# Graph attention on one core: the order of lower and whole sums, steps and masks at the end of a head

## The chip, the cores and the metric

The kernel runs on 1 core of a Trainium2 chip. The metric is the time of one execution on the device, in microseconds (us); lower is better. Several runs of each kernel are made, and their median is given.

## The reference, cut to what matters

Two layers are computed on x (4096 x 256) with one adjacency matrix of 4096 x 4096. The first layer is one graph attention and 30 steps of a small feed-forward network; the second is two graph attentions and a mixture of experts. Each of the three attentions has 4 heads of 64 columns:

```python
h = jnp.einsum('nd,mdo->mno', x, W)
e = jax.nn.leaky_relu(f_src[:, :, None] + f_dst[:, None, :], LEAK)
e = jnp.where(adj[None, :, :] > 0, e, NEG_INF)
attn = jax.nn.softmax(e, axis=-1)
out = jax.nn.elu(jnp.einsum('mnk,mko->mno', attn, h))
```

The change touches only how the three attentions are ordered.

## The kernel before, in words

**The trick of the attention.** The exponential of a leaky ReLU of a sum of two terms is one of two products, by the sign of the sum. So a neighbour k contributes to a row n with one of two prepared vectors, and which one is a comparison of 0 and 1. The kernel needs no exponential of a 4096 x 4096 matrix: it needs masks of 0 and 1 and matmuls of those masks with the prepared vectors (`vals`, 65 columns in two precision parts, an upper and a lower, for each of the two branches: 260 columns).

**Tiles and loops.** The 4096 rows are cut into chunks: of 4, 7, 7, 7 and 7 tiles of 128 rows in the first attention, and of 8, 8, 8, 8 in the second and third. For each chunk and head there are 16 units (q), each with 2 tiles of 128 neighbours. The list `units` runs over chunks, heads and q. So the first attention has 20 heads (chunk times head), the others 16 each, 52 in all. For each unit:

- ScalarE makes two steps (L466, tile `st`): large where the sum is positive, 0 elsewhere.
- VectorE makes a first mask `m1` (L580) from the step and the adjacency mask, and in 10 of 16 units a second mask `m2` (L604) as the difference of the adjacency mask and `m1`. In the other 6 units (`turned`) the vectors are prepared so that no second mask is needed.
- TensorE multiplies the masks with `vals` (L546) and accumulates over the 16 units into two PSUM tiles, `acc0` (4 tiles of rows, or fewer in the first chunk) and `acc1` (the others).

At a head's end ScalarE takes the lower part out of each accumulator, scaled (`lo`, L474, the "lower sum"), and VectorE adds it to the upper part (`u`, L475, the "whole sum"). Only then can the next head accumulate into the same tile. Below, lo0 and W0 are the lower and the whole sum of `acc0`, lo1 and W1 those of `acc1`. Then `close` works the sums to the head's output, in six pieces spread over the units that follow (L483 to L498, L638 to L642). In the first attention, during all chunks but the last, GpSimd also issues loads of the adjacency matrix for the next chunk (L209), TensorE turns them (L219), VectorE compares them (L227, L229) and SP stores them.

**What sets the order.** The main loop over `at` is written out by hand for VectorE and ScalarE (`tc.manual_schedule`): these two engines run their instructions in the order of the code. TensorE's order is left to the scheduler, which follows the code closely. An iteration issues the steps of unit `at + LEAD` (LEAD is 2), the masks of unit `at`, and the products of unit `at - LAG` (LAG is 1 in the first attention, 2 in the others). The step tiles have 3 buffers in the first attention and 4 in the others, the `m1` tiles likewise, and each accumulator one. When `at - LAG` is the first unit of a head, the sums of the head before are issued in this iteration, by `take`, once for k = 0 and once for k = 1.

Of the kernel before, what the change touches and what calls it, by code (L numbers as in the profile page):

```python
# [11 lines left out]
F32 = mybir.dt.float32  # L12
BF16 = mybir.dt.bfloat16
F16 = mybir.dt.float16
I32 = mybir.dt.int32
AF = mybir.ActivationFunctionType
OP = mybir.AluOpType
# [4 lines left out]
P = 128  # L22
# [9 lines left out]
DV = D + 1  # L32
BIG = 2.0**60
SCALE = 2.0**-4
LOW = 2.0**11
# [9 lines left out]
def gnn_ffn_kernel(ctx: ExitStack, tc: tile.TileContext, a: dict, out: bass.AP):  # L45
    nc = tc.nc
# [41 lines left out]
    def rows_in():  # L88
        return stream.tile([P, G * C], F32, name="rows")
# [35 lines left out]
    def turned(q):  # L125
        return q % 3 == 0
# [45 lines left out]
    def attention(tag, src, norm, w, others, chunks, first, ends, following):  # L172
# [6 lines left out]
        CM = max(chunks)  # L179
        with ExitStack() as scope:  # L180
# [3 lines left out]
            f2b = lay.tile([P, NT, H], F32, name="f2b")  # L184
# [4 lines left out]
            end = None if first else scope.enter_context(tc.tile_pool(name=f"{tag}_end", bufs=1))  # L189
            masks, arow, f1b = {}, {}, {}  # L190
# [53 lines left out]
            with ExitStack() as ps:  # L244
                prep = ps.enter_context(tc.tile_pool(name=f"{tag}_prep", bufs=1))
                work = ps.enter_context(tc.tile_pool(name=f"{tag}_pw", bufs=2))
# [204 lines left out]
            if first:  # L451
                end = scope.enter_context(tc.tile_pool(name=f"{tag}_end", bufs=1))
                made = scope.enter_context(tc.tile_pool(name=f"{tag}_made", bufs=2))
            work = scope.enter_context(tc.tile_pool(name=f"{tag}_work", bufs=2))
# [3 lines left out]
            units = [(c, h, q) for c in range(len(chunks)) for h in range(H) for q in range(NJ)]  # L458
            steps, accs = {}, {}

            def step_of(c, h, q):

                w = chunks[c] * P
                st = steps[c, h, q] = work.tile([P, 2, CM * P], BF16, name="st", bufs=3 if first else 4)
                for s in range(2):
                    nc.scalar.activation(  # L466
                        st[:, s, :w], f1b[c, h][:, :w], AF.Relu, bias=f2b[:, 2 * q + s, h : h + 1], scale=BIG
                    )

            def take(u, i0, n, acc):  # L470

                both = acc[:, :n, : 4 * DV].rearrange("p i (b s c) -> p i b s c", b=2, s=2)
                lo = end.tile([P, 4, 2, DV], F32, name="lo", bufs=2)
                nc.scalar.activation(lo[:, :n], both[:, :, :, 1, :], AF.Copy, scale=1.0 / LOW)  # L474
                nc.vector.tensor_tensor(u[:, i0 : i0 + n], both[:, :, :, 0, :], lo[:, :n], OP.add)  # L475

            def close(c, h, u):

                nt, t0 = chunks[c], starts[c]
                begin, finish = ends  # L480
                more = begin(t0, nt, h, end)
                v = u[:, :, 0, :]
                nc.vector.tensor_tensor(  # L483
                    v[:, :nt], v[:, :nt], r[:, t0 : t0 + nt, h : h + 1].to_broadcast([P, nt, DV]), OP.mult
                )
                yield
                nc.vector.tensor_tensor(v[:, :nt], v[:, :nt], u[:, :nt, 1, :], OP.add)
                yield

                nc.vector.tensor_tensor(v[:, :nt], v[:, :nt], hs[:, :, h, :].to_broadcast([P, nt, DV]), OP.add)  # L490
                z = end.tile([P, CM, 1], F32, name="z", bufs=2)
                nc.vector.reciprocal(z[:, :nt], v[:, :nt, D : D + 1])
                yield
                o = v[:, :, :D]
                nc.vector.tensor_tensor(o[:, :nt], v[:, :nt, :D], z[:, :nt].to_broadcast([P, nt, D]), OP.mult)
                yield
                e = end.tile([P, CM, D], F32, name="e")
                nc.scalar.activation(e[:, :nt], o[:, :nt], AF.Exp)  # L498
                yield
                finish(t0, nt, h, o[:, :nt], e[:, :nt], more)  # L500
                yield
# [25 lines left out]
            LEAD, LAG = 2, 1 if first else 2  # L527
            pairs = {}
# [34 lines left out]
            closing, making = None, None  # L563
            with tc.manual_schedule(engines={mybir.EngineType.DVE, mybir.EngineType.Activation}):
                for at in range(LEAD):
                    step_of(*units[at])
                for at in range(len(units) + LAG):
                    if at < len(units):
                        c, h, q = units[at]
                        w = chunks[c] * P  # L570
                        if q == 0 and h == 0 and first and c + 1 < len(chunks):
                            making = make(c + 1)
                        if q == 4 and at + NJ < len(units):
                            load_f1(*units[at + NJ - 4][:2])
                        if at + LEAD < len(units):
                            step_of(*units[at + LEAD])
                        m = masks[c, q // 4][:, 2 * (q % 4) : 2 * (q % 4) + 2, :w]
                        st = steps.pop((c, h, q))
                        m1 = work.tile([P, 2, CM * P], BF16, name="m1", bufs=3 if first else 4)
                        nc.vector.tensor_tensor(  # L580
                            m1[:, :, :w], st[:, :, :w], m, OP.logical_and if turned(q) else OP.min
                        )
                        pairs[at] = [m, m1, None]
                    for k in range(2):
                        b = at - LAG
                        if b >= 0:
                            bc, bh, bq = units[b]
                            if bq == 0:
                                if b:
                                    pc, ph_ = units[b - 1][:2]  # L590
                                    if k == 0:
                                        u = end.tile([P, CM, 2, DV], F32, name="u")
                                    take(u, *accs[pc, ph_][k])
                                    if k == 1:
                                        closing = close(pc, ph_, u)
                                        accs.pop((pc, ph_))
                                space(bc, bh, k)
                            products(b, k)
                        if k == 0 and at < len(units) and not turned(q):
                            if first:  # L600
                                m2 = work.tile([P, 2, CM * P], BF16, name="m2")
                            else:
                                m2 = rows_in().bitcast(BF16).rearrange("p (s n) -> p s n", s=2)
                            nc.vector.tensor_tensor(m2[:, :, :w], m, m1[:, :, :w], OP.subtract)  # L604
                            pairs[at][2] = m2
                    if b >= 0:
                        pairs.pop(b)
                        if bh == H - 1 and bq % 4 == 3 and bc + 1 < len(chunks):
                            load_mask(bc + 1, bq // 4)
                        if bq in (1, 2, 3, 4, 6, 8) and closing is not None:  # L610
                            next(closing)
                    if making is not None:
                        next(making, None)
                    if at == len(units) - (8 if first else 4):
                        for g in range(3 if first else 2):
                            load_ahead(*following[:1], g, *following[1:])
            c, h, q = units[-1]
            u = end.tile([P, CM, 2, DV], F32, name="u")
            for k in range(2):
                take(u, *accs[c, h][k])  # L620
            for _ in close(c, h, u):
                pass

# [35 lines left out]
    with ExitStack() as scope:  # L659
        one = scope.enter_context(tc.tile_pool(name="f_one", bufs=1))  # L660
        wT = one.tile([P, KC, C], F32, name="wT")
        bias = one.tile([P, C], F32, name="bias")
        last = one.tile([P, C], F32, name="last")
        y = one.tile([P, NT, C], F32, name="y")
        work = scope.enter_context(tc.tile_pool(name="f_work", bufs=3))
# [61 lines left out]
        units = FFN_STEPS * NG  # L727
        for at in range(units + 4):
# [18 lines left out]
            if 0 <= at - 3 < units:  # L747
                u = at - 3
# [13 lines left out]
                end = u >= units - NG  # L762
# [30 lines left out]
    for i in range(2):  # L793
        at = 1 + i * KC * E
# [29 lines left out]
    with ExitStack() as scope:  # L824
# [5 lines left out]
        acc = one.tile([P, NT, C], F32, name="acc")  # L830
# [10 lines left out]
        with ExitStack() as rs:  # L841
            work = rs.enter_context(tc.tile_pool(name="r_work", bufs=2))
# [15 lines left out]
            for g in range(NG + 2):  # L858
# [12 lines left out]
                if 1 <= g <= NG:  # L871
                    u = g - 1
# [4 lines left out]
                    n = work.tile([P, G, C], F32, name="n")  # L877
# [8 lines left out]
                if 2 <= g:  # L886
                    u = g - 2
# [18 lines left out]
            def numbers(name, pattern, base, step, dtype=F32):  # L906
# [19 lines left out]
            before = rone.tile([P, P], F32, name="before")  # L926
            nc.gpsimd.memset(before, 1.0)
            nc.gpsimd.affine_select(
                before, before, pattern=[[1, P]], compare_op=OP.is_gt, fill=0.0, base=0, channel_multiplier=-1
# [66 lines left out]
            first = rone.tile([P, E], F32, name="first")  # L996
# [19 lines left out]
            lo = rone.tile([P, 2, NT], F16, name="lo")  # L1016
# [3 lines left out]
            for b in range(2 * NT // HB):  # L1020
                i, t0 = b // 2, b % 2 * HB
# [152 lines left out]
        for i in range(T + 1):  # L1174
# [9 lines left out]
            h = hT.pop(i, None)  # L1184
# [55 lines left out]
```

## Time and profile before

| | us |
|---|---|
| median of 3 runs | 3596.79 (3593.67 to 3600.78) |
| the profiled execution | 3587.08 |
| its span | 3585.3 |
| first attention, first lower sum to last | 151.8 to 833.9 |
| second attention, the same | 2050.3 to 2593.3 |
| third attention, the same | 2696.8 to 3244.5 |

The profile is of one execution, a little faster than the three runs. Its times of instructions are read from the start of the span. Engines are PE (TensorE), PEld (its weight loads), DVE (VectorE), ACT (ScalarE), POOL (GpSimd) and SP (SyncE). A group of instructions is named by its line, engine and operation, with output and inputs by the program's tile names; "idle before, releaser" is the time for which the engine had nothing to run in front of the instruction, and what ended it. The ends of matmuls are modelled, and neighbouring instructions on one engine overlap a little, so that starts are the safer numbers.

### The profile page before, as it was taken

What the parts mean: (1) busy time and instruction counts of PE and PEld (TensorE: products, weight loads), DVE (VectorE), ACT (ScalarE), POOL (GpSimd) and SP (SyncE); (2) the same over time, 40 slices, a digit from 0 to 9 for tenths busy, and PEclk for the clock granted to TensorE, in tenths of its full rate; (3) what the DMA queues carried; (4) which work ended last, traced back from release to release, by engine and by line L of the source; (5) the groups of instructions that cost most, each with busy time, mean ns of one, the idle gap of its engine ahead of it and who ended that gap; (6) DMA issues with size and microseconds to landing.
All of it is one profiled execution on the core that took longest, in us unless ns stands there. A gap on an engine that the chain in (4) does not pass through costs nothing. (4 is left out here: it accounts for less than half of the span.)

```text
span 3585.3 us, 80790 instructions
## 1 busy us (share of the span) xinstructions
PE 3265.5 (91%) x33523; PEld 2971.2 (83%) x33523; DVE 3013.9 (84%) x6039; ACT 2612.6 (73%) x2902; POOL 1101.1 (31%) x899
## 2 busy tenths in 40 slices
PE   6789999987999999999998899999979999996895
PEld 5688888886888888888887799999868999994784
DVE  6789999987877877877787799999989999997445
ACT  2688888896766666666663799999879999993221
POOL 3210010003877777777772000000000000001663
PEclk8899999998999999999999899999999999998897
DMA  6796877601000000000006021303130331404224
GB/s 136 138 230 118 204 171 152 191 22 54 7 1 1 1 1 1 1 1 1 1 1 213 19 73 68 116 25 116 56 123 26 121 117 37 131 20 165 82 94 183
DMA packets 280199, 288.46 MB, mean 80 GB/s; under 512 B 97149, under 2 KB 230426, under 8 KB 279834
## 3 DMA queue, kind: packets, MB, share of 16 engines
q1 hardware_dynamic: 198770, 224.18, 18.9%
q0 software_dynamic: 73920, 52.97, 9.6%
q10 hardware_dynamic: 7144, 6.16, 0.6%
q8 instruction: 264, 4.33, 0.5%
q14 instruction: 101, 0.83, 0.1%
HBM read 248.01 MB, written 68.81 MB: 88 GB/s over the span
## 5 line engine op out<-in xcount | busy, mean ns | idle before, releaser
L546 PE MATMUL acc<-vals,m 128*128 128x130 f16 (+1 forms) x19456 | 1723.4, 233 | 138.1 <-DVE u L475 81.8
L466 ACT ACTIVATE st<-f1b,f2b 128x1024 bf16<-128x1024 f32 (+2 forms) x1664 | 1658.5, 1072 | 146.1 <-DVE m L580 138.2
L546 PEld LDWEIGHTS <-m 128*128 128x128 bf16 x19456 | 1525.2, 98 | 232.2 <-issue 85.7
L580 DVE TENSOR_TENSOR m<-st,m 128x2048 bf16<-128x2048 bf16 (+2 forms) x832 | 929.3, 1134 | 16.3 <-ACT st L466 12.4
L754 PE MATMUL po<-wT,zT 128*128 128x256 f32 x3840 | 875.2, 381 | 12.7 <-ACT zT L780 12.3
L754 PEld LDWEIGHTS po<-wT,zT 128*128 128x128 f32 x3840 | 714.0, 191 | 103.9 <-ACT zT L780 14.8
L740 POOL TENSOR_TENSOR th<-th,y 128x1024 f32<-128x1024 f32 x240 | 567.9, 2367 | 194.1 <-ACT th L739 193.5
L546 PE MATMUL acc<-vals,rows 128*128 128x130 f16 x5120 | 611.1, 221 | 0.0
L106 POOL TENSOR_TENSOR ln_rstd<-ln_rstd,mhalf 128x4 f32<-128x4 f32 x272 | 282.5, 1040 | 896.4 <-DVE ln_rstd L105 685.8
L101 DVE BATCH_NORM_STATS2 ln_st<-z 128x6 f32<-128x256 f32 x960 | 337.7, 413 | 191.3 <-ACT z L745 191.3
L546 PEld LDWEIGHTS <-rows 128*128 128x128 bf16 x5120 | 490.8, 96 | 0.4
L780 ACT COPY zT<-tp 128x1024 f32<-128x1024 f32 x240 | 243.0, 1012 | 323.8 <-PE tp L114 323.8
L604 DVE TENSOR_TENSOR rows<-m,m 128x2048 bf16<-128x2048 bf16 x320 | 391.7, 1224 | 10.2
L764 DVE SCALAR_TENSOR_TENSOR y<-po,ln_rstd,bias 128x256 f32<-128x256 f32 x928 | 378.2, 468 | 4.9 <-PE po L754 4.9
L745 ACT ACTIVATE z<-th 128x1024 f32<-128x1024 f32 x240 | 254.3, 1060 | 18.1 <-POOL th L740 17.8
L114 PE MATMUL tp<-ident,z 128*128 128x128 f32 x1920 | 250.8, 274 | 9.0 <-ACT z L745 8.0
L114 PEld LDWEIGHTS tp<-ident,z 128*128 128x128 f32 x1920 | 225.6, 141 | 35.7 <-ACT z L745 10.7
L739 ACT ACTIVATE th<-y 128x1024 f32<-128x1024 f32 x240 | 251.1, 1047 | 4.7 <-DVE y L764 4.7
L209 POOL DMA_DIRECT2D rows<-in_adj_dram x80 | 72.9, 912 | 510.1 <-PE tp_m L219 499.8
L604 DVE TENSOR_TENSOR m<-m,m 128x1792 bf16<-128x1792 bf16 (+1 forms) x200 | 202.2, 1011 | 12.7
L449 POOL MEMSET hs<- 128x4 f32 x3 | 0.3, 101 | 617.6 <-DVE u L490 596.4
L307 PE MATMUL ph<-g_w,xT 128*128 128x264 f32 x384 | 117.5, 469 | 31.1 <-DVE v L377 27.9
(212 smaller groups left out, 2312.9 us busy)
## 6 DMA issues: line engine op xcount, KB each, us to landing
m<-edges SPq DMA_DIRECT2D x32, 2048.0 KB, 9.8
rows<-in_adj_dram POOLq DMA_DIRECT2D x64, 448.0 KB, 7.1
edges<-ms SPq DMA_DIRECT2D x64, 448.0 KB, 5.1
m<-edges SPq DMA_DIRECT2D x16, 1792.0 KB
f1b<-fd SPq DMA_DIRECT2D x32, 512.0 KB, 3.5
rows<-x1d SPq DMA_DIRECT2D x16, 512.0 KB, 6.8
y<-yd SPq DMA_DIRECT2D x16, 512.0 KB, 9.0
f1b<-fd SPq DMA_DIRECT2D x16, 448.0 KB, 3.7
```

The source lines that it names most:

```text
L101: nc.vector.bn_stats(st[:, r, :], src[:, r, :])
L106: nc.gpsimd.tensor_tensor(rstd, rstd, mhalf, OP.pow)
L114: nc.tensor.transpose(ps[:, k, r * P : (r + 1) * P], src[:, r, k * P : (k + 1) * P], ident)
L466: nc.scalar.activation(st[:, s, :w], f1b[c, h][:, :w], AF.Relu, bias=f2b[:, 2 * q + s, h : h + 1], scale=BIG)
L546: nc.tensor.matmul(acc[:, i, cols], lhs[:, s, rows], v[:, cols], start=(j == 0 and n_ == 0), stop=(j == NT - 1 and n_ == 1), skip_group_ch ...
L580: nc.vector.tensor_tensor(m1[:, :, :w], st[:, :, :w], m, OP.logical_and if turned(q) else OP.min)
L604: nc.vector.tensor_tensor(m2[:, :, :w], m, m1[:, :, :w], OP.subtract)
L739: nc.scalar.activation(th[at], y[:, g * G : (g + 1) * G, :], AF.Tanh, scale=0.01)
L740: nc.gpsimd.tensor_tensor(th[at], th[at], y[:, g * G : (g + 1) * G, :], OP.add)
L745: nc.scalar.activation(z, th.pop(at - 1), AF.Silu, scale=0.01)
L754: nc.tensor.matmul(po[:, r, :], src[:, k, r * P : (r + 1) * P], wT[:, k, :], start=(k == 0), stop=(k == KC - 1),)
L764: nc.vector.scalar_tensor_tensor(y[:, g * G + r, :], po[:, r, :], rstd[:, r : r + 1], last if end else bias, op0=OP.mult, op1=OP.add,)
```

## The change

`take` is split in two, `lower_sums` (ScalarE) and `whole_sums` (VectorE), and `step_of` issues one step at a time. In the iteration of a head's end the order becomes:

| engine | before | after |
|---|---|---|
| ScalarE | step, step, lo0, lo1 | lo0, step, lo1, step |
| VectorE, first attention | m1, W0, m2, W1 | m1, W0, W1, m2 |
| VectorE, second and third | m1, W0, m2, W1 | W0, m1, W1, m2 |

In all other iterations the order is as before. The products of both halves are now written behind all of these. In the second and third attention this leaves TensorE's order as it was; in the first, at a head's start, the scheduler no longer puts the first matmuls of the second unit in front of `acc1`'s matmuls of the first. The orders of SP and GpSimd are the same. The number of buffers, the tiles and the arithmetic are unchanged, and so is the end of each attention behind the loop.

```diff
+                    b = at - LAG
+                    bc, bh, bq = units[b] if b >= 0 else (0, 0, -1)
+                    before = units[b - 1][:2] if b > 0 and bq == 0 else None
...
-                        if at + LEAD < len(units):
-                            step_of(*units[at + LEAD])
+
+                    los = []
+                    for k in range(2):
+                        if before:
+                            los.append(lower_sums(*accs[before][k]))
+                        step_of(at + LEAD, k)
+
+                    if before and not first:
+                        whole_sums(u, los[0], *accs[before][0])
...
                         pairs[at] = [m, m1, None]
-                    for k in range(2):
-                        b = at - LAG
-                        if b >= 0:
-                            bc, bh, bq = units[b]
+                    if before:
+                        if first:
+                            whole_sums(u, los[0], *accs[before][0])
+                        whole_sums(u, los[1], *accs[before][1])
+                        accs.pop(before)
+                        closing = close(*before, u)
+                    if at < len(units) and not turned(q):
...
+                        nc.vector.tensor_tensor(m2[:, :, :w], m, m1[:, :, :w], OP.subtract)
+                        pairs[at][2] = m2
+
+                    if b >= 0:
+                        for k in range(2):
                             if bq == 0:
-                                if b:
-                                    pc, ph_ = units[b - 1][:2]
-                                    if k == 0:
-                                        u = end.tile([P, CM, 2, DV], F32, name="u")
-                                    take(u, *accs[pc, ph_][k])
-                                    if k == 1:
-                                        closing = close(pc, ph_, u)
-                                        accs.pop((pc, ph_))
                                 space(bc, bh, k)
                             products(b, k)
-                        if k == 0 and at < len(units) and not turned(q):
...
-                            nc.vector.tensor_tensor(m2[:, :, :w], m, m1[:, :, :w], OP.subtract)
-                            pairs[at][2] = m2
```

The two functions that `take` was split into:

```python
def lower_sums(i0, n, acc):
    lo = end.tile([P, 4, 2, DV], F32, name="lo", bufs=2)
    nc.scalar.activation(lo[:, :n], split(acc, n)[:, :, :, 1, :], AF.Copy, scale=1.0 / LOW)
    return lo

def whole_sums(u, lo, i0, n, acc):
    nc.vector.tensor_tensor(
        u[:, i0 : i0 + n], split(acc, n)[:, :, :, 0, :], lo[:, :n], OP.add
    )
```

More of the change, by code (lines that the diff above doesn't have):

```diff
@@ L459, in attention, with step_of, split @@
             steps, accs = {}, {}
-            def step_of(c, h, q):
+            def step_of(at, s):
+                if at >= len(units):
+                    return
+                c, h, q = units[at]
                 w = chunks[c] * P
[L464 to L472, printed above, removed]
-                lo = end.tile([P, 4, 2, DV], F32, name="lo", bufs=2)
-                nc.scalar.activation(lo[:, :n], both[:, :, :, 1, :], AF.Copy, scale=1.0 / LOW)
-                nc.vector.tensor_tensor(u[:, i0 : i0 + n], both[:, :, :, 0, :], lo[:, :n], OP.add)
+                if s == 0:
+                    steps[at] = work.tile([P, 2, CM * P], BF16, name="st", bufs=3 if first else 4)
+                nc.scalar.activation(
+                    steps[at][:, s, :w], f1b[c, h][:, :w], AF.Relu, bias=f2b[:, 2 * q + s, h : h + 1], scale=BIG
+                )
+            def split(acc, n):
+                return acc[:, :n, : 4 * DV].rearrange("p i (b s c) -> p i b s c", b=2, s=2)
+            def lower_sums(i0, n, acc):
+                lo = end.tile([P, 4, 2, DV], F32, name="lo", bufs=2)
+                nc.scalar.activation(lo[:, :n], split(acc, n)[:, :, :, 1, :], AF.Copy, scale=1.0 / LOW)
+                return lo
+            def whole_sums(u, lo, i0, n, acc):
+                nc.vector.tensor_tensor(
+                    u[:, i0 : i0 + n], split(acc, n)[:, :, :, 0, :], lo[:, :n], OP.add
+                )
             def close(c, h, u):
@@ L565, in attention @@
                 for at in range(LEAD):
-                    step_of(*units[at])
+                    for s in range(2):
+                        step_of(at, s)
                 for at in range(len(units) + LAG):
+                    b = at - LAG
+                    bc, bh, bq = units[b] if b >= 0 else (0, 0, -1)
+                    before = units[b - 1][:2] if b > 0 and bq == 0 else None
+                    if before:
+                        u = end.tile([P, CM, 2, DV], F32, name="u")
                     if at < len(units):
@@ L574, in attention @@
                             load_f1(*units[at + NJ - 4][:2])
-                        if at + LEAD < len(units):
-                            step_of(*units[at + LEAD])
+                    los = []
[5 more added lines that the diff above has]
+                        whole_sums(u, los[0], *accs[before][0])
+                    if at < len(units):
                         m = masks[c, q // 4][:, 2 * (q % 4) : 2 * (q % 4) + 2, :w]
-                        st = steps.pop((c, h, q))
+                        st = steps.pop(at)
                         m1 = work.tile([P, 2, CM * P], BF16, name="m1", bufs=3 if first else 4)
@@ L583, in attention @@
                         pairs[at] = [m, m1, None]
-                    for k in range(2):
-                        b = at - LAG
-                        if b >= 0:
-                            bc, bh, bq = units[b]
-                            if bq == 0:
-                                if b:
-                                    pc, ph_ = units[b - 1][:2]
-                                    if k == 0:
-                                        u = end.tile([P, CM, 2, DV], F32, name="u")
-                                    take(u, *accs[pc, ph_][k])
-                                    if k == 1:
-                                        closing = close(pc, ph_, u)
-                                        accs.pop((pc, ph_))
+                    if before:
+                        if first:
[4 more added lines that the diff above has]
+                    if at < len(units) and not turned(q):
+                        if first:
+                            m2 = work.tile([P, 2, CM * P], BF16, name="m2")
+                        else:
+                            m2 = rows_in().bitcast(BF16).rearrange("p (s n) -> p s n", s=2)
+                        nc.vector.tensor_tensor(m2[:, :, :w], m, m1[:, :, :w], OP.subtract)
+                        pairs[at][2] = m2
+                    if b >= 0:
+                        for k in range(2):
+                            if bq == 0:
                                 space(bc, bh, k)
                             products(b, k)
-                        if k == 0 and at < len(units) and not turned(q):
[L600 to L604, printed above, removed]
-                            pairs[at][2] = m2
-                    if b >= 0:
                         pairs.pop(b)
@@ L619, in attention @@
             for k in range(2):
-                take(u, *accs[c, h][k])
+                whole_sums(u, lower_sums(*accs[c, h][k]), *accs[c, h][k])
             for _ in close(c, h, u):
```

## The prediction

> **What bounds the kernel now.** I read the page first (which engines are busy), then the table of windows for one head in each attention, then the timeline of one head's end, engine by engine, and last VectorE's list of waits by stage.
>
> The page's first part shows three engines close together, so no single one can be named from it:
> ```profile
> PE 3265.5 (91%) x33523; PEld 2971.2 (83%) x33523; DVE 3013.9 (84%) x6039; ACT 2612.6 (73%) x2902; POOL 1101.1 (31%) x899
> ```
> The windows below run from one first lower sum of a head to the next: the first attention, the second, the third. Columns: window, length, then busy us of TensorE, weight loads, VectorE, ScalarE, GpSimd, then clock, DMA share, GB/s.
> ```profile
> 424.88:463.17 38.29, 34.71 (x504) 32.32 (x504) 35.77 (x43) 32.18 (x36) 3.72 (x4) 1.00 0.64 122
> 2232.02:2268.13 36.11, 34.81 (x514) 33.35 (x512) 35.27 (x36) 35.10 (x36) 0.00 (x0) 1.00 0.08 24
> 2880.84:2917.22 36.38, 34.79 (x512) 33.33 (x512) 35.53 (x36) 35.09 (x36) 0.00 (x0) 1.00 0.11 31
> ```
> The reader is to see that VectorE works most in all three (35.77 of 38.29, 35.27 of 36.11, 35.53 of 36.38), and that the second and third attention have under 1.4 us of slack per head on any engine. What a head can win is what VectorE idles. The timeline of a head's end in the second attention (start, length, what, and in brackets the idle time before it and its releaser; ScalarE, then VectorE, then TensorE):
> ```profile
> 2227.87 4.25 ACT L466 ACTIVATE st<-f1b,f2b 128x1024 bf16<-128x1024 f32 x4
> 2232.03 1.07 ACT L474 ACTIVATE lo<-acc 128x520 f32<-128x520 f32 x2
> ...
> 2230.95 1.22 DVE L580 TENSOR_TENSOR m<-st,m 128x2048 bf16<-128x2048 bf16 x1
> 2232.64 0.70 DVE L475 TENSOR_TENSOR u<-acc,lo 128x520 f32<-128x520 f32 x1 [0.47 <-ACT lo L474]
> 2233.26 1.22 DVE L604 TENSOR_TENSOR rows<-m,m 128x2048 bf16<-128x2048 bf16 x1
> 2234.39 0.69 DVE L475 TENSOR_TENSOR u<-acc,lo 128x520 f32<-128x520 f32 x1
> ...
> 2229.25 2.84 PE L546 MATMUL acc<-vals,m 128*128 128x260 f16 x32
> 2233.39 1.56 PE L546 MATMUL acc<-vals,m 128*128 128x260 f16 x17 [1.30 <-DVE u L475]
> ```
> TensorE's last unit of the head runs 2229.25 to 2232.09; its first half of 16 matmuls (for acc0) is done 1.42 earlier, at 2230.67. The lower sum lo0 starts only at 2232.03, since the four steps before it fill ScalarE. So VectorE waits 0.47 and TensorE 1.30. VectorE's waits in the three attentions, in order (total us, times, longest):
> ```profile
> DVE u L475 <- ACT lo L474: 40.5, 20, 3.0
> ```
> ```profile
> DVE u L475 <- ACT lo L474: 14.1, 17, 3.8
> ```
> ```profile
> DVE u L475 <- ACT lo L474: 13.2, 16, 3.5
> ```
> That is 67.8 us in all: about 1.9 per head in the first attention, 0.47 and 0.45 in the others, except 3.1 at the first head's end of the second and third (timeline at 2050.9 and 2697.4). The last wait of each attention lies in the drain, where nothing is left to run: 3.0, 3.8 and 3.5 of the sum, and not to be won.
>
> **What the Trainium skill says.** "Trainium Architecture — The Big Picture", section "Inside one NeuronCore": every engine has an instruction stream of its own and meets the others only at semaphores. So the place of an instruction in its queue decides; the trace agrees (lo0 ready at 2230.67, run at 2232.03). "ScalarE: Activation LUTs", section "What ACT_TABLE_LOAD costs": an ACTIVATE with a pointer bias takes 280 ns + 0.833 ns per element, two in a row overlap by 93 ns: 1133 ns for a step of 1024, 1.04 us from start to start. The trace's median step is 1133 ns, and four take 4.25. "Perfetto Trace Analysis", section "Matmuls": groups should rotate through PSUM banks so that emptying one overlaps the next group. "PSUM — Partial Sum Buffer", section "PSUM: the matmul accumulator": 8 banks of 2 KiB a partition. Here acc0 and acc1 (4+4 tiles of 512 fp32) are all 8, so the only overlap is acc1's matmuls while acc0 is emptied.
>
> **The change part by part.** Nothing is added or removed: each engine has as many instructions as before, and the queues of SP and GpSimd keep their order. In the second and third attention TensorE's order stays too; in the first, at a head's start, the next unit's first few matmuls move behind those of acc1. What moves is 104 lower sums, 104 whole sums, the steps beside them, and the second masks (L604).
>
> *Second attention, a usual head.* ScalarE: lo0 moves past two steps, lo1 past one. The step in front of them ends at 2229.95 (two starts of 1.04 before 2232.03), so lo0 waits for TensorE until 2230.7 and ends at 2231.3; a step to 2232.3; lo1 (acc1 was done at 2232.09) to 2232.8; the other step to 2233.8. VectorE: W0 now stands ahead of the mask; 2231.3 to 2232.0, mask, W1 to 2233.8, second mask to 2234.9. TensorE starts at 2232.1 instead of 2233.39, and acc1 is free when it gets there. Already this first time the next mask starts at 2234.85 instead of 2235.00. From then on TensorE's head begins 1.1 us earlier against VectorE's queue: from W0's start it needs 0.70 + 0.06 + 33.4 (34.81 less the last half, 1.42) + 0.06 + 0.58 (lo0) + 0.03 = 34.8 us round to the next W0, ScalarE 35.1, VectorE 36.11 - 0.47 = 35.64. So VectorE sets the head, its wait is gone, and a head costs 35.64: **0.47 less**. ScalarE's wait for TensorE (0.75 at first) is hidden in what it already waits for buffers of VectorE (timeline: 0.72 at 2244.21, 0.93 per head in all).
>
> *Its first head's end.* lo0 comes 2.08 us (two steps) earlier, W0 at 2048.8 instead of 2050.86. The head after took 37.3, with 1.1 us in which VectorE waited for a buffer of the late TensorE; it takes 35.64 now. By the second head's end 3.7 us are won. With 13 more heads at 0.47: 3.7 + 6.1 = **9.8 us**.
>
> *Third attention.* In the same way: W0 2.08 earlier, the next head 38.56 down to 36.38 - 0.45 = 35.93: 4.7, and 13 x 0.45 = 5.9: **10.6 us**.
>
> *First attention.* There W0 stays behind the mask, and both whole sums come ahead of the second mask. Head end at 463 (chunks of 7 tiles): the step in front of lo0 ends 461.4, TensorE's acc0 at 461.4 (462.4 less 12 matmuls of 0.089), the mask 461.92. lo0 to 462.0, W0 462.03 to 462.73, a step, lo1 463.0 to 463.5, W1 463.5 to 464.06, second mask to 465.1, copy of the turned mask, next mask 465.53 instead of 466.41. VectorE's wait of 1.86 becomes 0.1 before W0 and 0.87 more before W1: **0.87 won**. TensorE starts at 462.9 instead of 464.54, and its next unit needs the second mask at 465.4, which is there at 465.1. The last chunk, which turns no masks, gives 0.93 by the same steps (wait 2.51 to 0.8 + 0.75), the first chunk's heads 0.58 and, where the chunk ends, 0.85. Sum: 3 x 0.58 + 0.85 + 11 x 0.87 + 4 x 0.93 = **15.9 us**. The last sums of each attention, which keep their order, I count at nothing: they wait for TensorE's last matmuls (ScalarE idle 5.7 us in front of lo0 at 832.9).
>
> The wait added: W1 waits for lo1, which stands behind a step, and the second mask is queued behind it, with TensorE's next unit waiting for that. It is 0.3 us early in the reckoning. The wait of a step behind lo0 isn't in the trace of before; its price lies between 0 (it replaces a wait for buffers) and 0.75 us per head. I take 0, since ScalarE has 1.0 us spare per head. DMA is not cover for anything: the share is 0.08 to 0.11 in usual heads of the later attentions; in a chunk's last head of the first attention it is 0.97, so four such heads might win nothing (3.5 us).
>
> **Sum:** 15.9 + 9.8 + 10.6 = 36.3 us. The profiled execution took 3587.08 (span 3585.3) and would take 3550.8; it was 9.7 under the median of 3596.79, so the median goes to **3560.5**.
>
> **The rivals.** (a) Main case as reckoned, gain 25 to 47: 0.70. (b) All of VectorE's waits for lower sums vanish, those before W1 too: 40.5 - 3.0, 9.7 + 0.6 and 9.1 + 1.6 (the buffer waits after the first heads), some 57 us, 3540. For it: TensorE would start 1.6 earlier per head. Against: lo1 stands behind a step of 0.94 in all of the first attention. 0.08. (c) Only the first attention wins, because in the others W0 ahead of the mask waits for TensorE as long as it did for ScalarE: 3596.8 - 15.9 = 3581. For it: 0.36 us of wait remains in the first reckoned head. Against: the loop over TensorE is 0.8 short of VectorE's. 0.10. (d) The wait is only handed on, from VectorE's sum to ScalarE's steps, and the head stays as long: no change, 3597. Over 1.0 us of spare time per head speaks against it. 0.05. (e) Slower, by one mechanism: lo0 blocks ScalarE until TensorE's acc0 is done, and the steps are queued behind it. ScalarE's head is 35.10 plus the stall; it decides from a stall of 1.01 us (second attention) or 1.29 (third), and outweighs the first attention's 15.9 from 1.7. With TensorE half a unit later (1.42) the stall is 2.14, a head 37.24, and 15 x 1.13 + 15 x 0.86 = 30 us are lost against 15.9 won: 3611. Against: TensorE is released earlier, not later. 0.07.
>
> **How the numbers follow.** About 0.2%, 7 us, is what a measurement of this kernel can tell from no change. (a), (b), (c) are faster: 0.88; (d) 0.05; (e) 0.07. The range 3538 to 3584 holds (a) and (b), (c), and some us of drift of the median (its runs span 7 us); it leaves out (d), (e) and some of the thinner gains.
>
> **What would show it.** Right: the wait of W0 near nothing in the later attentions, heads of 35.6 and 35.9 us there and some 37.4 in the first, TensorE's gap before a head under 1 us, ScalarE's lower sums with short waits for TensorE. Wrong: ScalarE busy 35.1 with waits over 1 us at lo0 and masks waiting for steps (e), or VectorE waiting 0.4 us and more before W0 in each later head (c), or TensorE waiting for the second mask after a head's start in the first attention.

## The result, and the profile after

The changed kernel took 3559.89 us (median of 4 runs, 3558.91 to 3561.31) against 3598.78 for the kernel before: a ratio of 0.9891, 95% interval 0.9873 to 0.9909. Measured again later, both kernels side by side, it was 3549.86 against 3583.46, a ratio of 0.9907 (0.9890 to 0.9924). About 1% is won, 34 to 39 us; 36.3 were predicted.

The page of the profile after, first part (busy us and share of the span, 3557.2 us):
```profile
PE 3272.9 (92%) x33523; PEld 2963.8 (83%) x33523; DVE 3010.9 (85%) x6039; ACT 2613.4 (73%) x2902; POOL 1101.7 (31%) x899
```
The work is the same, and the shares rose only because the span is shorter. The table of windows of the profile after, one head from lower sum to lower sum, in the first, second and third attention (window, length, busy us of PE, PEld, DVE, ACT, POOL, then clock, DMA share, GB/s):
```profile
414.94:452.34 37.40, 34.91 (x507) 32.27 (x506) 35.87 (x44) 32.28 (x35) 3.72 (x4) 1.00 0.64 125
2208.16:2243.71 35.55, 34.96 (x515) 33.34 (x514) 35.17 (x36) 35.10 (x35) 0.00 (x0) 1.00 0.09 24
2846.84:2882.65 35.81, 34.96 (x515) 33.32 (x514) 35.44 (x36) 35.10 (x35) 0.00 (x0) 1.00 0.11 31
```
A head fell from 38.29 to 37.40, from 36.11 to 35.55, from 36.38 to 35.81; VectorE is now busy for all but 0.4 us of a later head. Its list of waits in the second of these windows is empty: the 0.4 is made of 11 gaps of 0.03 us, each where an instruction uses the result of the one just before it. The timeline of the profile after at a head's end in the second attention (ScalarE, VectorE, TensorE):
```profile
2203.74 4.25 ACT L470 ACTIVATE st<-f1b,f2b 128x1024 bf16<-128x1024 f32 x4
2208.16 0.60 ACT L479 ACTIVATE lo<-acc 128x520 f32<-128x520 f32 x1 [0.17 <-PE acc L556]
2208.66 1.14 ACT L470 ACTIVATE st<-f1b,f2b 128x1024 bf16<-128x1024 f32 x1
2209.70 0.59 ACT L479 ACTIVATE lo<-acc 128x520 f32<-128x520 f32 x1
...
2207.77 1.23 DVE L619 TENSOR_TENSOR rows<-m,m 128x2048 bf16<-128x2048 bf16 x1
2208.91 0.69 DVE L483 TENSOR_TENSOR u<-acc,lo 128x520 f32<-128x520 f32 x1
...
2206.62 2.84 PE L556 MATMUL acc<-vals,m 128*128 128x260 f16 x32
2209.65 1.56 PE L556 MATMUL acc<-vals,m 128*128 128x260 f16 x17 [0.19 <-DVE u L483]
```
lo0 now runs 0.17 us after ScalarE is ready for it, released by TensorE itself, and W0 (2208.91) carries no wait. TensorE's gap is 0.19 instead of 1.30. VectorE's waits for lower sums in the three attentions of the profile after, in order (total us, times, longest):
```profile
DVE u L483 <- ACT lo L479: 22.8, 36, 3.0
...
DVE u L483 <- ACT lo L479: 6.0, 3, 3.2
...
DVE u L483 <- ACT lo L479: 5.5, 3, 3.2
```
Before they were 40.5, 14.1 and 13.2. In the later attentions only the first head's end and the last sums still wait, and in the third also the second head's end, for 0.17. In the first attention more than half is left, and the count rose from 20 to 36. The timeline of VectorE in the profile after, at a head's end there, tells why:
```profile
450.63 2.08 DVE L604 TENSOR_TENSOR m<-st,m 128x1792 bf16<-128x1792 bf16 x2
452.98 0.70 DVE L483 TENSOR_TENSOR u<-acc,lo 128x520 f32<-128x520 f32 x1 [0.26 <-ACT lo L479]
454.29 0.56 DVE L483 TENSOR_TENSOR u<-acc,lo 128x390 f32<-128x390 f32 x1 [0.62 <-ACT lo L479]
454.77 1.08 DVE L619 TENSOR_TENSOR m<-m,m 128x1792 bf16<-128x1792 bf16 x1
```
Both whole sums wait now, W0 for 0.26 and W1 for 0.62, with the second mask behind them.

By stage, from the traces, with the start of the last lower sum (lo1) of each attention as the mark (the second column holds the 30 steps of the feed-forward network too, and the last one the experts):

| us | to the end of the 1st attention | to the end of the 2nd | to the end of the 3rd | the rest | span |
|---|---|---|---|---|---|
| before | 833.9 | 1759.3 | 651.2 | 340.9 | 3585.3 |
| before, second profile | 835.8 | 1758.6 | 651.2 | 341.7 | 3587.4 |
| after | 815.6 | 1749.5 | 641.3 | 350.8 | 3557.2 |
| after, second profile | 815.1 | 1748.9 | 641.2 | 340.6 | 3545.7 |

The attentions gave 18.3, 9.9 and 9.9: 38.1 us. The first profile of after lost 10 of them again in the experts' stage. That is not the change: the second profile of the same kernel has no such loss.

### The profile page after: what moved, and what is told of

The parts are those of the page before. It is cut to its first block, busy times and chain, and to the rows that moved or that the text cites. A ratio compares the mean times of both kernels' runs of the same rounds, so it can differ in the third digit from the quotient of the medians.

```text
span 3557.2 us, 80784 instructions
## 1 busy us (share of the span) xinstructions
PE 3272.9 (92%) x33523; PEld 2963.8 (83%) x33523; DVE 3010.9 (85%) x6039; ACT 2613.4 (73%) x2902; POOL 1101.7 (31%) x899
## 5 line engine op out<-in xcount | busy, mean ns | idle before, releaser
L114 PEld LDWEIGHTS tp<-ident,z 128*128 128x128 f32 x1920 | 225.3, 141 | 35.5 <-ACT z L765 10.5
```

The lines of the kernel that those rows point to most:

```text
L114: nc.tensor.transpose(ps[:, k, r * P : (r + 1) * P], src[:, r, k * P : (k + 1) * P], ident)
```

## The experiments

My theory was that ScalarE's order was the whole loss, since lo0 stood behind two steps; the rivals gave the gain to VectorE's order, or to both together. Kernels that were measured together (a job) share runs of the kernel before, and it is the ratio to those that is compared. Each diff is against the changed kernel.

**ScalarE's order alone.** VectorE keeps the order of before.
```diff
-                    if before and not first:
-                        whole_sums(u, los[0], *accs[before][0])
 ...
-                    if before:
-                        if first:
-                            whole_sums(u, los[0], *accs[before][0])
-                        whole_sums(u, los[1], *accs[before][1])
 ...
+                                if before:
+                                    whole_sums(u, los[k], *accs[before][k])
                                 space(bc, bh, k)
                             products(b, k)
```


> ScalarE's order alone: lo0, step, lo1, step at a head's end, as in the changed kernel; VectorE keeps the order of before (mask, W0, second mask, W1). Theory (the lower sums behind the steps were the whole loss, and W1's place in front of the second mask costs the first attention 0.87 us per head of new waiting): later heads as in the changed kernel, 35.6 and 35.8 us; first attention 36.5 us per head of 7 tiles instead of 37.4, 33.4 instead of 34.1 in the last chunk, 24.5 instead of 24.9 in the first; in all some 15 us under the changed kernel, 3545. Rival (VectorE's order is what wins, W0 in front of the mask): later heads stay at 36.1 and 36.4, first attention 38.3, 3590 or more. Second rival (both parts are needed): between the two kernels, some 3575.

Measured: 3540.39 us, ratio 0.9861 (0.9844 to 0.9877). Heads are 36.69 us in the first attention (33.44 in the last chunk), 35.56 and 35.82 in the others. So it is ahead of the changed kernel. It ran a second time, beside the changed kernel.

> ScalarE's order alone, a second time, now beside the changed kernel on the same chip. Theory: VectorE's new order costs the first attention 0.72 us per head of 7 tiles (36.69 against 37.41), so this is 8 to 10 us under the changed kernel in the same job. Rival (the 10 us between the two so far come from the expert stage): no difference of medians beyond 3 us.

Measured: 3538.21 against 3549.86 of the changed kernel in the same job, ratios to before 0.9864 (0.9847 to 0.9881) and 0.9907 (0.9890 to 0.9924): 11.7 us between the medians, a little more than expected. In the traces the third attention's last lower sum comes 9.2 us earlier (3196.0 against 3205.2); the first attention alone ends 10.4 us earlier. VectorE's timeline of this second run, at the same kind of head's end in the first attention:
```profile
449.30 0.70 DVE L483 TENSOR_TENSOR u<-acc,lo 128x520 f32<-128x520 f32 x1 [0.27 <-ACT lo L479]
449.92 1.08 DVE L621 TENSOR_TENSOR m<-m,m 128x1792 bf16<-128x1792 bf16 x1
450.92 0.56 DVE L483 TENSOR_TENSOR u<-acc,lo 128x390 f32<-128x390 f32 x1
```
While ScalarE makes the step and lo1, VectorE has the second mask to do, and W1 no longer waits. So the gain comes from ScalarE's order, and VectorE's new order takes 0.7 us per head of 7 tiles off it. The edit also puts the products back where they were written before, which in the first attention bears on TensorE's order; that this is not what wins the 0.7 us is seen below, where two kernels keep the changed kernel's products, lose W1's wait in part or whole, and win 0.4 and 0.95.

**VectorE's order alone.** ScalarE keeps step, step, lo0, lo1.
```diff
                     los = []
                     for k in range(2):
-                        if before:
-                            los.append(lower_sums(*accs[before][k]))
                         step_of(at + LEAD, k)
+                    for k in range(2):
+                        if before:
+                            los.append(lower_sums(*accs[before][k]))
```


> VectorE's order alone, as in the changed kernel; ScalarE keeps step, step, lo0, lo1. Theory (ScalarE's order is the cause): first attention unchanged at 38.3 us per head, since W0 still waits for lo0; in the second and third W0 now waits in front of the mask, 1.6 us instead of 0.47, so a head is some 1.1 us longer (37.2 and 37.5), 29 times: 3597 + 33 = 3630. Rival (VectorE's order wins): 3560 to 3575. Rival (both needed): 3597.

Measured: 3622.15 us, ratio 1.0092 (1.0075 to 1.0109): slower than before. The window of a head in the second attention, and VectorE's timeline at its end:
```profile
2236.98:2274.23 37.25, 34.96 (x512) 33.33 (x512) 35.27 (x35) 35.31 (x37) 0.00 (x0) 1.00 0.08 23
```
```profile
2237.59 0.70 DVE L483 TENSOR_TENSOR u<-acc,lo 128x520 f32<-128x520 f32 x1 [1.60 <-ACT lo L479]
2238.21 1.21 DVE L605 TENSOR_TENSOR m<-st,m 128x2048 bf16<-128x2048 bf16 x1
```
The wait of 1.60 is the old 0.47 and the mask that used to fill the time in front of it; a head takes 37.25, or 37.51 in the third attention, and 38.30 as ever in the first. The same VectorE order that is free in the changed kernel costs 1.14 us per later head if lo0 is late.

**lo0 moved up by one step instead of two**, with VectorE as before (its edit is that of the first experiment).
```diff
                     for k in range(2):
-                        if before:
-                            los.append(lower_sums(*accs[before][k]))
                         step_of(at + LEAD, k)
+                        if before:
+                            los.append(lower_sums(*accs[before][k]))
```


> VectorE as before; ScalarE: step, lo0, step, lo1, so lo0 moves up by one step (1.04 us, 0.93 in the first attention) instead of two. Theory (VectorE waits for as long as lo0 stands behind steps, no matter what else): in the later attentions one step is more than the wait of 0.47, so the heads are 35.56 and 35.82 as with two steps; in the first attention the wait of 1.86 falls by 0.93 only, heads of 7 tiles 37.3 to 37.4, last chunk 34.1; in all some 10 us over ScalarE's order alone. Rival (what counts is that TensorE restarts early): the later heads lose part of the gain, 35.8 and 36.1.

Measured: 3551.57 us, ratio 0.9913 (0.9896 to 0.9929). Windows of a head in the three attentions:
```profile
454.65:492.00 37.35, 34.64 (x507) 32.33 (x505) 35.76 (x43) 32.17 (x36) 3.74 (x4) 1.00 0.67 125
2206.34:2241.88 35.54, 34.80 (x515) 33.35 (x513) 35.16 (x37) 35.11 (x37) 0.00 (x0) 1.00 0.09 24
2846.68:2882.49 35.81, 34.82 (x516) 33.36 (x514) 35.43 (x37) 35.10 (x37) 0.00 (x0) 1.00 0.12 31
```
As the theory had it: where VectorE's wait was shorter than a step, one step is enough; where it was 1.86 us, half is left. When TensorE restarts does not matter by itself here: its gap before a head of the second attention is 0.7 us instead of the changed kernel's 0.2, and the head is as short.

**Both lower sums in front of both steps**, the rest as in the changed kernel. It tests the slower rival of the prediction, and whether lo1's place made W1 wait.
```diff
                         if before:
                             los.append(lower_sums(*accs[before][k]))
+                    for k in range(2):
                         step_of(at + LEAD, k)
```


> The changed kernel with both lower sums in front of both steps: lo0, lo1, step, step. Theory (in the first attention W1 waits for lo1 because that stands behind a step): W1's wait falls from 0.87 to some 0.35 us, heads of 7 tiles 36.9 us; in the later attentions lo1 makes ScalarE wait 0.75 us for TensorE's last matmuls, which its spare time hides; in all 3552. Rival (e of the prediction: a lower sum in front of the steps holds ScalarE and the masks behind it wait): the later heads get 0.3 to 0.4 us longer, 35.9 and 36.2, in all 3564 or more.

Measured: 3541.81 us (3538.85 to 3550.77), ratio 0.9863 (0.9846 to 0.9879). Heads of 7 tiles in the first attention are 36.98 us instead of 37.40, and W1's wait there is 0.20 instead of 0.62, so lo1's place did make W1 wait. The heads of the others are 35.56 and 35.82, as in the changed kernel. The window of a head in the second attention, and ScalarE's list of waits in it, which has one line:
```profile
2210.47:2246.03 35.56, 34.98 (x515) 33.33 (x513) 35.19 (x36) 34.88 (x37) 0.00 (x0) 1.00 0.08 24
```
```profile
ACT lo L479 <- PE acc L556: 0.7, 1, 0.7
```
ScalarE does stand still for the 0.7 us, with the steps queued behind, and the head is not longer by any of it: the slower rival is wrong at this size. But 34.88 and 0.68 of waiting make the whole 35.56, so in the second attention ScalarE has nothing left; a longer stall is not tested. The profiled execution, 3550.77, was the slowest of its four, and its stretch from the first attention's end to the second's is 6 us longer than in the changed kernel, with the same heads.

**Both whole sums behind both masks in the first attention**, the rest as in the changed kernel.
```diff
-                    if before:
-                        if first:
-                            whole_sums(u, los[0], *accs[before][0])
+                    if before and not first:
                         whole_sums(u, los[1], *accs[before][1])
 ...
                         pairs[at][2] = m2
+                    if before:
+                        if first:
+                            for k in range(2):
+                                whole_sums(u, los[k], *accs[before][k])
```


> The changed kernel, with both whole sums behind both masks in the first attention (m1, m2, W0, W1), so that VectorE has the second mask to do while lo0 and lo1 are made. Theory (VectorE's waits set the first attention's heads): no wait left, heads of 7 tiles 36.4 instead of 37.41, last chunk 32.8 instead of 34.14, some 15 us under the changed kernel and 5 under ScalarE's order alone. Rival (TensorE, which then restarts 0.9 us later than with ScalarE's order alone, becomes the bound): heads of 36.7 and more, 33.4 and more in the last chunk, nothing under ScalarE's order alone.

Measured: 3537.40 us, ratio 0.9860 (0.9841 to 0.9879), not to be told from ScalarE's order alone. Heads of 7 tiles are 36.45 us, 33.13 in the last chunk. In a usual head of 7 tiles VectorE waits for no lower sum any more:
```profile
450.81 1.09 DVE L615 TENSOR_TENSOR m<-m,m 128x1792 bf16<-128x1792 bf16 x1
451.82 1.16 DVE L483 TENSOR_TENSOR u<-acc,lo 128x520 f32<-128x520 f32 x2
452.90 0.61 DVE L229 TENSOR_SCALAR ms<-tp_m 128x896 bf16<-128x896 bf16 x1
```
The last chunk missed the 32.8 that was expected: there W1 still waits 0.47. The first attention's heads are shorter than with ScalarE's order alone by a further 0.2 to 0.3 us, some 3 us from its first lower sum to its last, about as much as two executions differ elsewhere. So the rival, TensorE as the bound, does not hold for the heads, though the medians are the same.

**Less work for VectorE.** One addition of `close` is left out.
```diff
-                nc.vector.tensor_tensor(v[:, :nt], v[:, :nt], hs[:, :, h, :].to_broadcast([P, nt, DV]), OP.add)
```


> The changed kernel without one addition on VectorE per head: the small sum hs, which is added to the head's numerator and denominator, is left out, so the output lacks it. It is 0.69 us of VectorE's time per head (0.63 in the first attention), in a place where no other engine waits for it. Theory (since the change VectorE sets a head's length in all three attentions): the heads get shorter by nearly that much, down to what ScalarE needs: 35.1 to 35.2 us in the second and third attention instead of 35.55 and 35.81, 36.8 instead of 37.4 in the first. Rival (ScalarE or TensorE sets it already): the heads of the later attentions stay at 35.5 and 35.8.

One execution: 3516.14 us, beside 3585.47 for the kernel before. Windows of a head of the second and third attention:
```profile
2193.04:2227.92 34.88, 34.80 (x515) 33.34 (x514) 34.54 (x35) 34.88 (x35) 0.00 (x0) 1.00 0.08 24
2820.93:2855.99 35.06, 34.87 (x515) 33.33 (x514) 34.72 (x35) 34.90 (x35) 0.00 (x0) 1.00 0.12 32
```
A head lost 0.67 us in the second attention and 0.75 in the third, the whole addition; in the first attention 0.69. So VectorE set the length of the changed kernel's heads. Here ScalarE (34.88) and TensorE (34.80) fill the second attention's head as well, and the next shortening would have to take from all three. ScalarE's need had been put at 35.1, its busy time in the longer heads; it is smaller, since steps that follow each other without a gap overlap.

**The two kernels again**, for the 10 us in the experts' stage.

> The kernel before, unchanged, for a second profile. In the first profile of before the 36 expert tiles at the end follow each other by 5.62 us throughout; in the profile of the changed kernel every second one takes some 6.1, and the end is 10 us longer. Theory (this changes from run to run and has nothing to do with the change): the attentions end at the same times as in the first profile of before (833.9, 2593.3, 3244.5), and where the time is near 3597 the expert tiles alternate as in the changed kernel. Rival (the change lengthens the expert stage): tiles of 5.62 throughout although the time is near 3597, with the lost time elsewhere.

> The changed kernel, unchanged, beside the kernels of this call. Theory (the 10 us at the end of its first profile come and go from run to run): attentions end as in its first profile (815.6, 2565.1, 3206.4), the expert tiles may follow each other by 5.62 us throughout, and then the execution takes some 3549. Rival (the change itself makes the expert stage longer): the tiles alternate between 5.62 and 6.1 again.

Measured: 3589.09 us for before, with the experts' tiles 5.62 us apart and the rest in 341.7; the attentions end 1 to 2 us later than in the first profile. After, in its second profile: tiles 5.62 apart, the rest in 340.6, the execution 3547.46. In all other profiles of this study the rest took 340.5 to 343.2; only in the first one of after was every second tile some 6.1 us. The change does not bring it, since the same kernel has it in one profile and not in the other. Whether it goes with the execution or with the job was not found.

## Why the prediction was right, point by point

- **The mechanism** (lo0 ready, but queued behind two steps, and VectorE the bound that waits for it): right. One step instead of two, and VectorE's order alone, each moved the heads as the reckoning said, and the shorter VectorE work showed the bound.
- **A usual later head**, 35.64 and 35.93 predicted, measured 35.56 and 35.82. The 0.1 more is the step that counted idle time only: the trace's 0.47 runs from the mask's end, while two instructions with no wait between them overlap (W0 to the next is 0.62 for 0.70). Counted from start to start, 2230.95 to 2232.64 is 1.69, where a mask followed without a wait takes 1.14: 0.55.
- **The first heads' ends**: right. Counted from the attention's first step, lo0 comes 2.08 us earlier in both (41.60 instead of 43.68), as reckoned, and the next lo0 comes 3.96 us earlier in the second attention (3.7 predicted) and 4.45 in the third (4.7).
- **The last heads** were left out of the sum, as if they stayed at 34.9. They now take as long as the others, 35.57 and 35.82, and gave back 0.7 and 0.9 us. From its first step on, the second attention won 10.5 and the third 10.9, where 9.8 and 10.6 were predicted; the table has 9.9 for both, as 0.7 and 1.0 us were lost in the stretches in front of their first steps. Why those got longer was not followed up.
- **The first attention**: 0.87 per head of 7 tiles predicted and 0.89 measured, 0.93 and 0.91 in the last chunk, 0.58 and 0.67 in the first; 15.9 against 18.3 in all. Of the difference 0.6 lies in front of the attention's first step, and most of the rest at the first chunk's end, where two heads fell by 2.9 instead of 1.7. The heads at a chunk's end, which might have won nothing because of their DMA, won 0.9 like the others (38.74 to 37.87). The new wait was foreseen in its sum (0.97, measured 0.26 + 0.62) and in its place, and the second mask behind it; that it made VectorE's half of the change a loss there was in the numbers and was not said.
- **ScalarE's wait for TensorE**, taken at nothing: right, up to 0.7 us per head. **The slower rival** (e) did not come: ScalarE's wait was 0.17 in a usual later head. Its reckoning was also too high, since 35.10 plus a stall of 0.7 would be 35.8, and the head with that stall took 35.56. **Rival (b)** did not come: 22.8 of the first attention's 40.5 us of waits stayed. **Rival (c)** did not come: W0 ahead of the mask waits for nothing in a usual later head. **Rival (d)** did not come: every usual head got shorter.
- **Slips in the numbers**, none of which carries the result: the third attention's usual wait is 0.47 too, not 0.45; with it the waits of (b) sum to some 58 us instead of 57; TensorE's slack in a head of the third attention is 1.6 us, not under 1.4; and of the 104 sums of each kind, the six at the attentions' ends do not move.
- **The sum against the clock.** The predicted 3560.5 met the median of 3559.89 more closely than the reasoning deserves: the profiled execution of before was 10 us under its median, and that of after had 10 us more in the experts' stage. The medians of before in three jobs were 3598.78, 3591.73 and 3583.46, so the ratio is the sounder measure: 0.9899 predicted, 0.9891 and 0.9907 measured. That the predicted time was met to within 1 us is luck.

## What to carry to other kernels

In a hand-written order, put an instruction that frees a single buffer ahead of work that is only made in advance, and count how long it stands behind such work: the gain ends where that wait ends. The consumer's order is another matter: give the waiting engine something to do between two results that arrive one after the other, and do not queue its needed work behind a wait. Try the two halves of such a change apart, since one may pay for the other; here ScalarE's half alone was 11.7 us better than both.

## What was not expected of the hardware

An engine's wait can cost more than the idle time shown, by the overlap that the two instructions around it lose: 0.55 us of a head for an idle time of 0.47. The same overlap is missing on VectorE where an instruction uses the result of the one just before it: in a head of the second attention of the profile after, such an instruction starts 0.03 us after the end of the one before, and every other one 0.08 us before that end.
